# First transfers, layer seam and constants of a four-layer graph network reordered on one core

## Chip, cores and metric

The kernel runs on one core of a Trainium2 chip. The metric is the device time of one execution in microseconds (us), as the median of several executions. All arithmetic is 32-bit float.

## The reference, cut to what matters

128 graphs of 64 nodes with 256 features pass through four layers. Each layer's output is added to its input and the sum is layer-normalised.

```python
x = LN(x + L0(x, adj))    # 5 node groups: two graph convolutions 256 -> 512 -> 256, weighted by a softmax
x = LN(x + L1(x, adj))    # one graph convolution, 256 -> 256
x = LN(x + L2(x, adj))    # polynomial of degree 3 in the row-normalised adjacency, leaky relu
x = LN(x + L3(x, adj))    # 5 steps of a gated recurrent unit over A = (adj != 0)

# L0, per group g with its nodes idx (25, 9, 7, 6 and 6 of the 64):
A = adj_g + I;  An = dinv * A * dinv
h = relu(An @ (x_g @ W1[g]) + b1[g])
fused[idx] += w[g] * relu(An @ (h @ W2[g]) + b2[g])
# L3: agg = A^T (h W_l);  h = GRU(agg, h)   for l in 0..4
```

## The kernel before

Layer 0 works on 8 batches of 16 graphs. Layers 1 to 3 work on 16 chunks of 8 graphs. Layer 0's result of a chunk goes through DRAM (`x1`). The engines' transfers are issued in order, each by the queue of the engine that the call names (`nc.sync`, `nc.scalar`, `nc.gpsimd`).

```python
def load0(s):                                 # 18 adjacency and 12 row transfers per batch
    for t, (g, b0, nb) in enumerate(TILES):
        for f, n in RUNS[g]:
            for fc, m in RUNS[g]:
                nc.sync.dma_start(a0[s % 2][rows, t, col : col + m], adj[b, f : f + n, fc : fc + m])
            nc.sync.dma_start(xg[rows, t, :], x[b, f : f + n, :])
    # ... two 512 KB tiles xt of the inputs for the residual, on nc.sync
loaded = {0: load0(0)}
# ... ident, eye0, block0, b1 on nc.scalar
for g in range(NG):                           # 10 x 512 KB of weights
    nc.scalar.dma_start(W1[:, g], ...)
    nc.gpsimd.dma_start(W2[:, g], ...)
# ... b2, fusion weights fw on nc.sync

# prep(s):   ae = a0 + eye, degrees, A0 (VectorE); transposes pT; gathers pa0 -> ag0
# groups(s): hidden(g): ph -> hg;  support(g): ps -> s2;  add(g): po -> F (fusedT)
# residual(s): transposes pse of F, xt += pse, layernorm, store to x1
for _ in prep(0):
    pass
for s in range(NS):
    beside = []
    if s:
        beside.append(residual(s - 1))
    if s + 1 < NS:
        loaded[s + 1] = load0(s + 1)
        beside.append(prep(s + 1))
    interleave(*beside, groups(s))            # one step of each in turn
interleave(residual(NS - 1))

# after layer 0, in its memory: loads of chunks 0 and 1 (a64, xt), constants, then
interleave(both(mid(0), mid(1)), fold())      # mid: layers 1 and 2 of a chunk; fold: recurrent weights
for c in (0, 1):
    rows.append(Chunk(c)); rows[c].state_of_layer2(); rows[c].messages()
for s in range(NCH * L):                      # the recurrent loop, mid(c) of later chunks as filler
    ...
```

Of the kernel before, what the change touches and what calls it, by code (L numbers as in the profile page):

```python
# [43 lines left out]
def gnn_stack(  # L44
# [29 lines left out]
    small = ctx.enter_context(tc.tile_pool(name="small", bufs=4))  # L74
    dram = ctx.enter_context(tc.tile_pool(name="dram", bufs=1, space=bass.MemoryType.DRAM))
# [60 lines left out]


    with ExitStack() as c0:
        w0 = c0.enter_context(tc.tile_pool(name="w0", bufs=1))
        work = c0.enter_context(tc.tile_pool(name="work0", bufs=1))  # L140
        pt = c0.enter_context(tc.tile_pool(name="pt0", bufs=8, space=PSUM))

        def psum(name):
            return pt.tile([128, 512], F32, tag="pt", name=name)
# [6 lines left out]
        nc.gpsimd.memset(A0, 0.0)  # L151

        def load0(s):
            xg = work.tile([TR, NT, D], F32, name="xg", bufs=2)
            for t, (g, b0, nb) in enumerate(TILES):
                b = slice(s * SB + b0, s * SB + b0 + nb)
                row = 0
                for f, n in RUNS[g]:
                    rows = slice(row, row + nb * n)
                    row += nb * n  # L160
                    col = 0
                    for fc, m in RUNS[g]:
                        nc.sync.dma_start(a0[s % 2][rows, t, col : col + m], adj[b, f : f + n, fc : fc + m])
                        col += m
                    nc.sync.dma_start(xg[rows, t, :], x[b, f : f + n, :])
            xt = []
            for c in (2 * s, 2 * s + 1):
                t = work.tile([128, NP, D], F32, name="xt0", bufs=4)
                nc.sync.dma_start(t, xv[c])
                xt.append(t)  # L170
            return a0[s % 2], xg, xt

        loaded = {0: load0(0)}

        ident = const(c_ident, [128, 128], "ident", nc.scalar)
        eye0 = const(c_eye0, [TR, NT, NJ], "eye0", nc.scalar, w0)
# [4 lines left out]
        for g in range(NG):  # L181
            nc.scalar.dma_start(W1[:, g], w1[g].rearrange("(k p) e -> p k e", p=128))
            nc.gpsimd.dma_start(W2[:, g], w2[g].rearrange("(k p) e -> p k e", p=128))
        b2c = const(b2.rearrange("g (k p) -> p (g k)", p=128), [128, NG * 2], "b2", pool=w0)
# [22 lines left out]
        def prep(s):  # L207

            a, xg, xt = loaded.pop(s)
# [25 lines left out]
            for t0 in range(0, NT, 4):  # L235
                n = min(4, NT - t0)
                p = psum("pT")[:TR, : n * TR].rearrange("p (t n) -> p t n", t=n)
# [8 lines left out]
            for ts, o, w in ((range(4), 0, half), (range(4, NT), half, NC0 - half)):  # L246
                for k in range(2):
                    p = psum("pa0")
# [8 lines left out]
            ready[s] = AT, ag0, xt  # L257

        def groups(s):

            AT, ag0, xt = ready.pop(s)
# [6 lines left out]
            def hidden(g):  # L268
                _, o, w = at(g)
                hg = work.tile([128, 4, w], F32, name="hg0" if g == 0 else "hg", bufs=1 if g == 0 else 2)  # L270
                for e in range(4):
                    p = psum("ph")[:, :w]
# [7 lines left out]
            def support(g):  # L280
                ts, o, w = at(g)
                hg, s2 = hgs.pop(g), []
                for u in range(0, len(ts), 2):
                    tu = ts[u : u + 2]
                    p = psum("ps").rearrange("p (t d) -> p t d", t=2)
# [12 lines left out]
            def add(g):  # L298
# [3 lines left out]
                for k in range(2):  # L302
                    p = psum("po")[:, :w]
# [23 lines left out]
            ready[s, "x"] = xt  # L327

        def residual(s):
            for c, xt in zip((2 * s, 2 * s + 1), ready.pop((s, "x"))):  # L330
                for t in range(NP // 2):
                    p = psum("pse").rearrange("p (q d) -> p q d", q=2)
# [15 lines left out]
        for s in range(NS):  # L348
            beside = []
            if s:  # L350
                beside.append(residual(s - 1))
            if s + 1 < NS:
                loaded[s + 1] = load0(s + 1)
                beside.append(prep(s + 1))
            interleave(*beside, groups(s))
# [4 lines left out]
    pg = ctx.enter_context(tc.tile_pool(name="pg", bufs=5, space=PSUM))  # L360
    pt = ctx.enter_context(tc.tile_pool(name="pt", bufs=3, space=PSUM))

    def psum(name):
        return pt.tile([128, 512], F32, tag="pt", name=name)

    def load(c):
        a64 = work.tile([128, NP, N], F32, name="a64", bufs=2)
        nc.sync.dma_start(a64, av[c])
        xt = work.tile([128, NP, D], F32, name="xt", bufs=5)
        nc.sync.dma_start(xt, x1[c])  # L370
        return a64, xt

    loaded = {0: load(0), 1: load(1)}

    pair = const(c_pair, [128, 2, N], "pair", nc.scalar)
    cw = spread(conv_w, 4, "cw")
    cb = spread(conv_b, 1, "cb")
    l1bs = spread(l1b, D, "l1bs")
    L1W = const(l1w.rearrange("(k p) e -> p k e", p=128), [128, 2, D], "L1W")
    L2W = const(l2wT.rearrange("(k p) e -> p k e", p=128), [128, 2, D], "L2W")  # L380
    bih = const(bihT, [128, 6], "bih")
    bhh = const(bhhT, [128, 6], "bhh")
    mask = const(maskT, [128, B // 2], "mask")
    brz = wp.tile([128, 4], F32, name="brz")
    nc.vector.tensor_add(brz, bih[:, 0:4], bhh[:, 0:4])


    cI = wp.tile([128, 3, 128], F32, name="cI")
    for k in range(3):
        nc.vector.tensor_scalar(cI[:, k, :], ident, cw[:, k : k + 1], None, op0=ALU.mult)  # L390
# [3 lines left out]
    V = [wp.tile([128, 3, 7, 128], F32, name=f"V{l}") for l in range(L)]  # L394
    WHH = wp.tile([128, 3, 7, 128], F32, name="WHH")
# [8 lines left out]
    def fold():  # L404
        st = work.tile([128, 4, 2, D], F32, tag="RZ", name="ih", bufs=2)
        whh = work.tile([128, 2, 3 * D], F32, tag="NI", name="whh", bufs=2)
        for q in range(3):
            nc.gpsimd.dma_start(st[:, q], wihT[:, q * D : (q + 1) * D].rearrange("(k p) e -> p k e", p=128))
        nc.gpsimd.dma_start(whh, whhT.rearrange("(k p) e -> p k e", p=128))
        wl = work.tile([128, 4, 2, D], F32, tag="RZ", name="wl", bufs=2)  # L410
        wls = [wl[:, l] for l in range(4)] + [st[:, 3]]
        for l in range(L):
            nc.gpsimd.dma_start(wls[l], wlT[l].rearrange("(k p) e -> p k e", p=128))
        yield
# [6 lines left out]
        for l in range(L):  # L421
            for q in range(3):
                p = psum("pf").rearrange("p (j e) -> p j e", j=2)
                for j in range(2):
                    for k in range(2):
                        nc.tensor.matmul(
                            p[:, j, :], wls[l][:, k, j * 128 : (j + 1) * 128], st[:, q, k, :], start=k == 0, stop=k == 1
# [62 lines left out]
    def gather(src, m, name, tag="ag"):  # L490

        a = work.tile([128, 2, NP * 128], F32, tag=tag, name=name, bufs=2 if tag == "agg" else 1)
        for k in range(2):
            p = psum("pa")
            for q in range(NP):
                nc.tensor.matmul(  # L496
                    p[:, q * 128 : (q + 1) * 128], src[:, q, k * 128 : (k + 1) * 128], m[:, q, :], start=True, stop=True
                )
            nc.scalar.copy(a[:, k, :], p)  # L499
        return a  # L500

    state = {}

    def mid(c):

        a64, xt = loaded.pop(c)


        Ab = work.tile([128, NP, 128], F32, name="Ab", bufs=1)
        nc.vector.tensor_mul(  # L510
            Ab.rearrange("p q (b m) -> p q b m", b=2),
            a64[:, :, None, :].to_broadcast([128, NP, 2, N]),
            pair[:, None, :, :].to_broadcast([128, NP, 2, N]),
        )
        A01 = work.tile([128, NP, 128], F32, name="A01", bufs=4)
        nc.vector.tensor_scalar(A01, Ab, 0.0, None, op0=ALU.not_equal)
        rsum = small.tile([128, NP], F32, name="rsum")
        nc.vector.tensor_reduce(rsum, a64, AX.X, ALU.add)
        rdeg = small.tile([128, NP], F32, name="rdeg")
        nc.vector.tensor_scalar(rdeg, rsum, 1.0, None, op0=ALU.add)  # L520
        rinv = small.tile([128, NP], F32, name="rinv")
        nc.vector.tensor_scalar(rinv, rsum, 1e-9, None, op0=ALU.add)
        nc.vector.reciprocal(rinv, rinv)
        dinv1 = inv_sqrt(rdeg, NP, 128, "d1")
        A1 = work.tile([128, NP, 128], F32, name="A1", bufs=1)
        nc.vector.tensor_add(A1, Ab, ident[:, None, :].to_broadcast([128, NP, 128]))
        nc.vector.tensor_mul(A1, A1, dinv1[:, :, None].to_broadcast([128, NP, 128]))
        nc.vector.tensor_mul(Ab, Ab, rinv[:, :, None].to_broadcast([128, NP, 128]))
        yield


        AT1 = work.tile([128, NP, 128], F32, name="AT1", bufs=1)
        p = psum("pT1").rearrange("p (q n) -> p q n", q=NP)
        for q in range(NP):
            nc.tensor.transpose(p[:, q, :], A1[:, q, :], ident)
        nc.vector.tensor_mul(AT1, p, dinv1[:, :, None].to_broadcast([128, NP, 128]))

        poly = work.tile([128, NP, 128], F32, tag="poly", name="poly3", bufs=2)
        p = psum("pT2").rearrange("p (q n) -> p q n", q=NP)
        for q in range(NP):  # L540
            nc.tensor.transpose(p[:, q, :], Ab[:, q, :], ident)
        nc.vector.scalar_tensor_tensor(
            poly, p, cw[:, 3:4], cI[:, 2, None, :].to_broadcast([128, NP, 128]), op0=ALU.mult, op1=ALU.add
        )
        yield
# [139 lines left out]
    def both(*gens):  # L685
        for g in gens:
            yield from g
# [120 lines left out]
```

## Time and profile before

| | before |
|---|---|
| median (lowest to highest of 3) | 2464.16 us (2463.45 to 2464.48) |
| span of the profiled run | 2462.4 us, mean granted clock 0.986 |
| busy share | TensorE 93%, VectorE 53%, ScalarE 44%, GpSimd 23% |
| first transposes of batch one / batch two | 38.99 us / 61.73 us |
| layer 0 in the middle (61.73 to 338.66) | 276.9 us |
| seam: last batch to the loop's first gate product (338.66 to 484.80) | 146.1 us, TensorE busy 104.1 |
| recurrent loop (from 484.80) | 1977.6 us |

The last four rows cut the span at batch two's transposes, the last batch and the loop, without gaps. The granted clock is TensorE's clock in the profile as a share of full speed. TensorE's idle time lies densest at the start (38.99 and 4.36 us) and in the seam (42.0 of 146.1 us). The loop has 86.3 us of it in 1977.6, which the change does not aim at. The lines behind the table are shown in the prediction.

### The profile page before, as it was taken

Reading aid. Unit: us, or ns where it says so; the run is one execution under the profiler, and the core shown is the slowest. Engines: PE = TensorE matmul, PEld = TensorE weight load, DVE = VectorE, ACT = ScalarE, POOL = GpSimd, SP = SyncE. Lnnn points to the kernel's source line nnn. Section 1 sums busy time; section 2 is a strip of 40 time slices with the busy share of each in tenths; the row PEclk is TensorE's granted clock in tenths of the full one; section 3 lists DMA queues with packets and bytes.
Section 4 is the critical chain, followed back from the end, with each engine's and each line's share of the span. In section 5 each row is a group of like instructions: output and inputs, shape, how many; then the busy total and the mean of one; then the engine's idle time right before and its main releaser. Section 6 shows DMA issues by size and latency. Waiting matters only on the chain.

```text
span 2462.4 us, 31767 instructions
## 1 busy us (share of the span) xinstructions
PE 2281.0 (93%) x12288; PEld 1994.1 (81%) x12288; DVE 1315.6 (53%) x2914; ACT 1090.6 (44%) x2102; POOL 567.0 (23%) x606
## 2 busy tenths in 40 slices
PE   2999994999999999999999999999999999999996
PEld 2878783788888888888888888888888888888885
DVE  1333324555566556655565556555655565555445
ACT  1343441444444444444445444545454545454443
POOL 1101002322222222222222222222132222222221
PEclk9999996999999999999999999999999999999998
DMA  5222113000000000000000000000000000000000
GB/s 157 67 79 88 50 44 116 3 3 1 3 18 20 1 3 18 20 1 3 18 20 1 3 18 20 1 3 16 22 1 1 9 18 1 1 3 16 1 1 17
DMA packets 55318, 54.34 MB, mean 22 GB/s; under 512 B 24224, under 2 KB 48512, under 8 KB 55168
## 3 DMA queue, kind: packets, MB, share of 16 engines
q1 hardware_dynamic: 51616, 43.74, 5.6%
q0 software_dynamic: 1504, 5.51, 0.6%
q10 hardware_dynamic: 2048, 3.06, 0.4%
q8 instruction: 97, 1.59, 0.3%
q14 instruction: 53, 0.43, 0.1%
HBM read 35.52 MB, written 16.78 MB: 21 GB/s over the span
## 4 chain that ended last, share of the span: by engine, by line
PE 53%; DVE 29%; ACT 9%; POOL 3%; issue 3%; DMA 2%; SPq 1%; DVEq 0%; POOLq 0%; ACTq 0%
PE parz L460 9%; PE pan L460 6%; PE pa L496 6%; PE ps L289 5%; PE pdrz L460 4%; PE pbrz L460 4%; DVE RZ L653 4%; DVE RZ L654 4%; PE ph L274 4%; DVE hn L655 3%; DVE NI L647 2%; DVE NI L648 2%; ACT NI L652 2%; DVE RZ L482 2%; PE pbn L460 2%
## 5 line engine op out<-in xcount | busy, mean ns | idle before, releaser
L476 ACT COPY c<-parz 128x512 f32<-128x512 f32 x240 | 140.4, 585 | 369.9 <-PE parz L460 369.9
L460 PE MATMUL parz<-Th,WHH 128*128 128x256 f32 x960 | 285.9, 379 | 0.0
L460 PE MATMUL parz<-Ta,V 128*128 128x256 f32 x960 | 285.5, 379 | 0.0
L440 POOL TENSOR_TENSOR Th<-hn 128x512 f32<-128x512 f32 x64 | 93.5, 1461 | 653.5 <-DVE hn L655 653.5
L652 ACT ACTIVATE NI<-NI,bih 128x512 f32<-128x512 f32 x160 | 115.5, 722 | 224.4 <-DVE NI L648 224.4
L460 PEld LDWEIGHTS parz<-Ta,V 128*128 128x128 f32 x960 | 182.4, 190 | 24.8
L476 ACT COPY c<-pan 128x512 f32<-128x512 f32 x240 | 141.0, 587 | 125.9 <-PE pan L460 125.1
L440 POOL TENSOR_TENSOR Ta<-agg 128x512 f32<-128x512 f32 x80 | 101.5, 1269 | 400.8 <-ACT agg L499 400.8
L460 PEld LDWEIGHTS parz<-Th,WHH 128*128 128x128 f32 x960 | 176.0, 190 | 21.2 <-ACT c L476 0.5
L478 DVE TENSOR_TENSOR NI<-pdn,c 128x512 f32<-128x512 f32 x80 | 54.8, 684 | 229.8 <-ACT c L476 229.8
L460 PE MATMUL pan<-Ta,V 128*128 128x256 f32 x480 | 147.4, 389 | 20.9 <-ACT c L476 19.7
L625 ACT ACTIVATE RZ<-RZ,brz 128x512 f32<-128x512 f32 x160 | 106.4, 712 | 128.0 <-DVE RZ L488 128.0
L107 POOL TENSOR_TENSOR rs<-ve,mhalf 128x4 f32<-128x4 f32 x64 | 64.5, 1008 | 413.6 <-DVE ve L105 401.7
L460 PE MATMUL pan<-Th,WHH 128*128 128x256 f32 x480 | 143.7, 381 | 0.0
L482 DVE TENSOR_TENSOR NI<-pbn,c 128x512 f32<-128x512 f32 x80 | 55.3, 692 | 149.9 <-PE pbn L460 149.4
L496 PEld LDWEIGHTS pa<-A,h 128*128 128x128 f32 x1024 | 123.7, 192 | 13.9 <-ACT h L669 11.0
L113 ACT ACTIVATE xt<-xt,nb,rs 128x256 f32<-128x256 f32 x192 | 99.7, 589 | 75.3 <-DVE nb L110 75.3
L496 PE MATMUL pa<-A,h 128*128 128x128 f32 x1024 | 125.5, 276 | 7.7 <-ACT h L669 7.6
L289 PE MATMUL ps<-W,hg 128*100 128x256 f32 (+3 forms) x576 | 131.8, 381 | 0.0
L596 PE MATMUL pT<-ident,hn 128*128 128x128 f32 x640 | 96.5, 277 | 25.9 <-DVE hn L655 25.9
L596 PEld LDWEIGHTS pT<-ident,hn 128*128 128x128 f32 x640 | 74.2, 141 | 48.5 <-PE pT L596 34.3
L289 PEld LDWEIGHTS ps<-W,hg 128*100 128x100 f32 (+3 forms) x576 | 91.0, 163 | 27.2
(183 smaller groups left out, 5214.4 us busy)
## 6 DMA issues: line engine op xcount, KB each, us to landing
xt<-in_x_dram SPq DMA_DIRECT2D x16, 512.0 KB
x<-xt SPq DMA_DIRECT2D x16, 512.0 KB
xt<-x SPq DMA_DIRECT2D x16, 512.0 KB
out_dram<-xt SPq DMA_DIRECT2D x16, 512.0 KB
xg<-in_x_dram SPq DMA_DIRECT2D x32, 100.0 KB
W<-in_w_dram POOLq DMA_DIRECT2D x5, 512.0 KB, 9.2
W<-in_w_dram ACTq DMA_DIRECT2D x5, 512.0 KB
a<-in_adj_dram SPq DMA_DIRECT2D x16, 128.0 KB
```

The costliest lines, as they stand in the source:

```text
L113: nc.scalar.activation(y[:, p, :], y[:, p, :], AF.Identity, bias=nb[:, p : p + 1], scale=rs[:, p : p + 1])
L274: nc.tensor.matmul(p, W1[:, g, k, e * 128 : (e + 1) * 128], ag0[:, k, o : o + w], start=k == 0, stop=k == 1)
L289: nc.tensor.matmul(p[:r, h, :], hg[:, e, TOFF[t] - o : TOFF[t] - o + r], W2[:, g, e, :], start=e == 0, stop=e == 3,)
L440: nc.gpsimd.tensor_sub(t[:, 0:2, :], a[:, :, H:], a[:, 0, :].rearrange("p (s n) -> p s n", s=2))
L460: nc.tensor.matmul(bank[:, g, :], w[:, q, i - 1, :], rhs, start=i in (1, 2, 5) and g == 0 and m == 0, stop=m == len(side) - 1, skip_group_ ...
L476: nc.scalar.copy(c, self.a)
L482: nc.vector.tensor_add(C[:, :, 0, :H], b, self.copies.pop(1))
L496: nc.tensor.matmul(p[:, q * 128 : (q + 1) * 128], src[:, q, k * 128 : (k + 1) * 128], m[:, q, :], start=True, stop=True)
L596: nc.tensor.transpose(p[:, q * 128 : (q + 1) * 128], src(q, k), ident)
L625: nc.scalar.activation(RZ[:, q, 0, :], RZ[:, q, 0, :], AF.Sigmoid, bias=b[0])
L652: nc.scalar.activation(n, n, AF.Tanh, bias=bih[:, 4 + j : 5 + j])
L653: nc.vector.tensor_sub(d, self.hT[:, j, :], n)
```

## The change

Its intent has three parts. Batch one's transfers go out first, on three queues, and the weights follow on the sync queue. Layers 1 and 2 of the first two chunks run beside layer 0's last batch. The constants and the recurrent weights are fetched during layer 0, into memory of their own. The diff, with moved code and renamings cut:

```diff
+    keep = ctx.enter_context(tc.tile_pool(name="keep", bufs=1))    # mid, load, gather moved up and into keep
+    pg = ...(name="pg", bufs=5, space=PSUM)                        # PSUM: 8 buffers become 5 + 3
+    pt = ...(name="pt", bufs=3, space=PSUM)
...
         def load0(s):
+            qa = [nc.scalar, nc.sync] if s == 0 else [nc.sync]
+            qx = nc.gpsimd if s == 0 else nc.sync
...
-                        nc.sync.dma_start(a0[s % 2][rows, t, col : col + m], ...)
+                        qa[i % len(qa)].dma_start(a0[s % 2][rows, t, col : col + m], ...)
-                    nc.sync.dma_start(xg[rows, t, :], x[b, f : f + n, :])
+                    qx.dma_start(xg[rows, t, :], x[b, f : f + n, :])
...
         for g in range(NG):
-            nc.scalar.dma_start(W1[:, g], ...)
-            nc.gpsimd.dma_start(W2[:, g], ...)
+            nc.sync.dma_start(W1[:, g], ...)
+            nc.sync.dma_start(W2[:, g], ...)
+        xts = {0: load_x(0)}
...
             if s + 1 < NS:
                 packed[s + 1] = load0(s + 1)
+                xts[s + 1] = load_x(s + 1)
                 beside.append(prep(s + 1))
+            if s == 1:
+                pair = const(..., nc.gpsimd)        # and cw, cb, l1bs; L1W, L2W, bih, bhh, mask on nc.gpsimd
...
+            elif s == 3:                            # wihT, whhT, wlT: 9 transfers, 2.8 MB, on nc.gpsimd
+                nc.gpsimd.dma_start(ih[:, q], ...)
...
+            elif s == NS - 1:
+                for c in (0, 1):
+                    loaded[c] = load(c)
+                beside.append(both(mid(0), mid(1)))
             interleave(*beside, groups(s))
...
-        interleave(both(mid(0), mid(1)), fold())
+        weights = fold()
         for c in (0, 1):
+            for _ in range(6):
+                next(weights)
             rows.append(Chunk(c))
             ...
+        for _ in weights:
+            pass
```

## The prediction

> **What bounds the kernel now.** I read the table of busy time by stretch first, cut at the instructions that begin and end the stages, then the waits of TensorE in the bad stretch, then the timeline around its edges. The columns of the first are: stretch in us, its length, busy time of TensorE's matmuls, its weight loads, VectorE, ScalarE and GpSimd (instructions in brackets), granted TensorE clock, DMA share, GB/s.
>
> ```profile
> 0.00:38.99 38.99, 0.00 (x0) 0.03 (x1) 2.92 (x11) 0.00 (x0) 8.62 (x12) 1.00 0.65 197
> 38.99:61.73 22.74, 18.39 (x77) 14.99 (x78) 5.47 (x24) 7.43 (x14) 1.80 (x1) 0.99 0.31 89
> ...
> 338.66:374.22 35.56, 34.34 (x205) 27.97 (x205) 10.79 (x37) 14.84 (x36) 2.01 (x2) 1.00 0.07 30
> 374.22:484.80 110.58, 69.78 (x360) 61.79 (x361) 60.94 (x196) 31.05 (x86) 30.66 (x42) 0.80 0.19 66
> 484.80:2462.40 1977.60, 1891.28 (x9954) 1665.10 (x9952) 1141.32 (x2304) 922.43 (x1694) 501.04 (x532) 0.99 0.03 9
> ```
>
> The recurrent loop (from 484.80, 80% of the span) has TensorE busy 1891 of 1978 us. The change does not touch its instructions, so 1977.6 us stay. Layer 0 between 61.73 and 374.22 is just as full (34.3 of 35.6 us in its last batch). What is to be had lies in two places: the start, where TensorE does nothing for 38.99 us, and the seam from 374.22 (layer 0's last transposes) to 484.80 (first gate product of the loop), where it is idle for 40.8 us of 110.6 and its mean clock is 0.80.
>
> TensorE's waits in the seam (engine, tile and line, whom it waited for: total us, times, longest):
>
> ```profile
> PE pT L535 <- DVE d1z L89: 19.8, 1, 19.8
> PE pa L496 <- ACT xt L113: 11.6, 2, 6.7
> PE pa L496 <- DVE AT L536: 7.6, 2, 7.3
> PE pp L550 <- DVE poly L552: 1.8, 2, 0.9
> ```
>
> The 19.8 us are layer 0's last layernorm, its store, then the loads of the first chunk and the weights, which only now have room. The 11.6 us are the two layernorms of layer 1, on which the second gather depends, and there is little else for TensorE to do.
>
> The timeline at the start (start us, length, engine, what, and the idle time before it):
>
> ```profile
> 5.45 19.96 ACTq L182 DMA_DIRECT2D W<-in_w_dram  x5
> ...
> 34.50 0.40 DVE L211 TENSOR_TENSOR ae<-a,eye 112x225 f32<-112x225 f32 x1 [33.12 <-DMA a<-in_adj_dram]
> ...
> 38.99 1.90 PE L239 MATMUL pT<-ident,A 112*112 112x112 f32 x9 [38.99 <-DVE A L219]
> ...
> 57.23 0.40 DVE L211 TENSOR_TENSOR ae<-a,eye 112x225 f32<-112x225 f32 x1 [14.61 <-DMA a<-in_adj_dram]
> ...
> 61.73 1.90 PE L239 MATMUL pT<-ident,A 112*112 112x112 f32 x9 [4.36 <-DVE A L219]
> ```
>
> The first batch's 30 small transfers share the engines with 5.2 MB of weights and are there at 34.50. The second batch's 30 follow on the sync queue from 36.97 and are there at 57.23: 20.3 us for 0.9 MB, one issue per 0.65 us, so the queue's issuing sets this. TensorE had finished the first batch's hidden layer at 57.37 and waited 4.36 us for batch two's transposes, although batch one's next products were ready.
>
> **What the Trainium skill says.** "TensorE: Matmul & The Clock Gate", Part 1 (the HAM clock gate): the array's clock falls to half after an idle window of some 3.4 us and comes back after a busy one. The trace agrees: after the 19.8 us wait the gather of 16 matmuls took 3.78 us, after a wait of 4.95 us 3.98 us, and 2.05 us where TensorE had been busy. The same page, Part 2, Step-by-step: matmuls stay in program order; only weight loads are pulled ahead. The 4.36 us above agree, so I let TensorE follow the program. "DMA: Bandwidth & Descriptors", Issuing engines are not separate DMA queues: transfers from several issuers run on the same 16 DMA engines, so a second issuer saves issue time only. The page calls that usually small; here it is 20 us for a batch, so three queues do help batch one, but the bytes of the weights must still pass.
>
> **The change, part by part.**
>
> *Start.* Batch one: 9 adjacency issues each on two queues at 0.65 us (5.9 us from 0.75), 12 row issues on GpSimd at some 0.75 us (its weight issues took 0.748 us). Landing takes about 1.5 us (last issue of batch two ended at 55.8, the sum began at 57.23), with a weight transfer possibly ahead. The sum could begin near 11, the transposes 4.5 us later as before (34.50 to 38.99), delayed by GpSimd, which now clears a tile after its 12 issues: near 16. The hidden layer began 9.5 us after the transposes and ended 8.9 us later, so TensorE is through with it at 34 to 36 instead of 57.37. That would be 22 us won.
>
> But batch two's transposes come next in the program, and batch two's transfers stand on the sync queue behind all weights and two input tiles. Bytes ahead: 10 x 512 KB and 2 x 512 KB are 6.3 MB, batch one's rows 0.87 MB, constants 0.36 MB, together 7.5 MB. The DMA engines moved 350 GB/s where they were full (10 to 15 us), so 21.5 us, from about 2 us on: done at 24. I choose that 6 of batch two's 30 issues are out by then; 24 x 0.65 = 15.6 us makes 39.6, plus 1.5 to land and 4.5 to the transposes: 46. TensorE idles about 11 us where it idled 4.36, and **61.7 becomes about 46: 15.5 us won, not 22.**
>
> *Seam.* The two chunks' layers 1 and 2 move beside layer 0's last batch. Their TensorE work at full clock, from the second chunk's groups: transposes 1.0, gathers 2 x 2.05, polynomial 2 x 1.15, linear layers 2 x 3.62: 14.7 us each, 29.4 for both. Stage from 338.66, summed anew: the last batch 35.6 (it has no next batch to prepare), plus 29.4. Waits that stay, in program order: after each first linear layer comes only one piece of layer 0 (1.9 us) before the second gather, but the layernorm takes 6.7 us (415.7 to 422.4, 448.8 to 455.4), so 2 x 4.8; the polynomial 2 x 0.9; two half-clock gathers 2 x 1.9; 1 for other things: 16 us. Then the last transposes 1.9, the folded weights 15 x 1.75 = 26.2 (40 matmuls took 8.80 us), both chunks' transposes and gathers 5.6 (479.23 to 484.80). Sum 114.7 against 146.1 before (338.66 to 484.80). I take off 1.5 for PSUM, as layer 0's eight buffers are now 5 and 3, the 3 shared with the moved work: **30 us won.**
>
> *Constants.* The small ones already went out at 144 to 148 us, in layer 0, so moving them gives nothing. The 2.8 MB of recurrent weights, which had to wait at 389 for layer 0's memory, now come 200 us early; that gain is in the seam's sum (the weights are resident when the folding begins). GpSimd pays 9 issues at 0.75 us, beside 44 us stages that use 2 to 6 us of it: hidden.
>
> Total 45.5 of 2464.2: **2419 us**, 1.8% less.
>
> **Rivals.** (a) The start wins all: if batch two is there by 36, because the sync queue pushes it between the weights, 25 us are won and the time is about 2409. Against it: the queue is served in order and its issue rate is seen. (b) The start wins nothing: the weights crawl as from 15 to 30 us, when the same DMA engines ran half full at 148 to 218 GB/s; then they end at 35, batch two at 58, and the time is 2434. For it: that stretch; against it: there the weights competed with 100-row transfers on their own queue, and only one weight queue ran. (c) The moved work fits better: if TensorE's order fills the layernorm waits, the seam wins 41 us, and the time is 2408. Against it: the order above shows no such filling. (d) VectorE becomes the bound in the last batch: it has 10.8 us there and would take some 40 more in about 80, so no, but its queue may lengthen each layernorm by 1 to 3 us and cost 2 to 6: 2424.
>
> **Range and chances.** Start 15.5 give or take 6, seam 30 give or take 6, taken as independent: give or take 8.5, and a little wider for the order of the queues, which I cannot see. 8 in 10: 2404 to 2435. The 2% line is 2414.9, that is 49.3 us won; I stand 4 us short of it, so faster by over 2% has 0.33, within 2% 0.65, slower 0.02.
>
> **What would show it.** First transposes near 16 us and batch two's near 46 with about 11 us of idle time before them, ended by VectorE after an adjacency transfer. Weights landed by about 24 at 340 GB/s or more. From the last batch's first transposes to the first gate product about 116 us, with two waits of 4 to 5 us of the second gathers on ScalarE's layernorm, and no wait near 20 us. The clock at 1.00 in the folding. The loop 1977 us long, within 3. The prediction is wrong if batch two's transposes are no later than batch one's hidden layer, if the weights' transfer is slower, or if the loop itself moves.

## The result, and the profile after

| | before | after |
|---|---|---|
| median (lowest to highest of 4) | 2463.80 us (2461.78 to 2464.48) | 2432.17 us (2431.15 to 2432.88) |
| ratio to before | | 0.9873 (95%: 0.9856 to 0.9890) |
| span of the profiled run, mean clock | 2462.4 us, 0.986 | 2429.4 us, 0.987 |

A ratio is the mean time of one kernel's fast runs over that of the other's of the same rounds, so it is not quite the ratio of the medians. The kernel is 1.3% faster, within 2%, and the time lies inside the stated range, 13 us above the stated 2419.

The table of busy time by stretch of the kernel after has the columns of the prediction's first view. It is cut at the same events: both first transposes, the last batch, layer 0's last transposes, the loop.

```profile
0.00:19.77 19.77, 0.00 (x1) 0.03 (x1) 2.93 (x11) 1.28 (x1) 13.90 (x22) 1.00 0.70 168
19.77:62.93 43.16, 18.56 (x77) 15.09 (x78) 5.72 (x25) 5.59 (x13) 10.05 (x14) 0.76 0.70 227
62.93:341.68 278.75, 269.50 (x1700) 225.58 (x1701) 99.34 (x370) 114.73 (x272) 26.25 (x21) 0.98 0.22 70
341.68:413.63 71.95, 62.74 (x377) 54.04 (x377) 41.36 (x122) 27.77 (x60) 7.18 (x8) 0.95 0.10 34
413.63:453.16 39.53, 37.14 (x185) 32.42 (x185) 27.99 (x81) 18.01 (x60) 23.93 (x32) 0.91 0.15 54
453.16:2429.40 1976.24, 1890.09 (x9953) 1664.69 (x9951) 1142.19 (x2308) 921.84 (x1696) 494.19 (x524) 1.00 0.03 9
```

The first transposes begin 19.2 us earlier, at 19.77 instead of 38.99. Batch two's begin at 62.93 instead of 61.73, so **all of that is gone one stage later**. The second line shows it: of 43.16 us TensorE is busy 18.56. Booked by piece, before to after:

| piece | before | after | difference | predicted |
|---|---|---|---|---|
| to batch two's transposes | 61.73 | 62.93 | +1.2 | -15.5 |
| to the last batch | 276.93 | 278.75 | +1.8 | 0 |
| seam | 146.14 | 111.48 | -34.7 | -30 |
| loop | 1977.60 | 1976.24 | -1.4 | 0 |
| sum (spans) | 2462.4 | 2429.4 | -33.0 | -45.5 |

TensorE's waits of the kernel after before the loop (whom it waited for: total us, times, longest):

```profile
PE pT L365 <- DVE A L345: 44.4, 2, 24.6
PE pse L461 <- DVE d1s L94: 6.5, 1, 6.5
PE pa L157 <- ACT xt L116: 5.5, 2, 4.3
PE pse L461 <- DVE fusedT L445: 4.6, 2, 3.5
PE pf L543 <- ACT w L550: 2.1, 1, 2.1
```

The first line is the start: 19.77 us before batch one and 24.60 before batch two. The second line is new. The third is what is left of the two layernorm waits of 11.6 us, and the wait of 19.8 us at the seam is gone.

Where the 24.60 us come from is in the timeline of the transfers' issues and of the instructions that wait for them (kernel after; start us, length, engine, line, what, count, idle time before it):

```profile
1.25 10.15 ACTq L284 DMA_DIRECT2D a<-in_adj_dram  x9
1.25 11.73 SPq L284 DMA_DIRECT2D a<-in_adj_dram  x9
...
18.39 0.79 POOL L82 DMA_DIRECT2D L1W<-in_l1w_dram  x1
...
22.43 11.08 SPq L294 DMA_DIRECT2D xt<-in_x_dram  x2
...
26.34 2.88 POOL L508 DMA_DIRECT2D wl<-in_wlT_dram  x4 [0.39 <-DMA L2W<-in_l2wT_dram]
...
35.87 0.68 SPq L284 DMA_DIRECT2D a<-in_adj_dram  x1
...
58.40 0.40 DVE L337 TENSOR_TENSOR ae<-a,eye 112x225 f32<-112x225 f32 x1 [14.37 <-DMA a<-in_adj_dram]
```

Three things are to be seen. First, two queues need 10.15 and 11.73 us for 9 adjacency issues each, so 1.1 to 1.3 us for one, where one of batch two's in the kernel before took 0.65. The weights after the first stand behind these issues on the sync queue, and the second weight leaves only at 13.03. Second, GpSimd's queue sends `L1W` at 18.39 and `wl` at 26.34, with the other later weights between. The program names them in its second and fourth stage (`s == 1`, `s == 3`), but nothing made these issues wait, and they were placed as early as they could go. Third, the sync queue's two `xt` issues take 11.08 us, so batch two's first issue leaves at 35.87 and its last near 57.

The view of the DMA queues between 13 and 36 us says how much that was (packets, MB, share of the 16 engines):

```profile
q1 hardware_dynamic: 3426, 4.29, 56.3%
q0 software_dynamic: 946, 3.13, 37.4%
```

The second line is GpSimd's queue: 3.13 MB of constants and weights of layers 1 to 3, which TensorE first uses after 341 us (3.5 MB were issued in all; the rest moved after 36 us). In this stretch 333 GB/s are moved, so by this estimate they cost 3.13 MB / 333 GB/s = 9.4 us of full DMA engines. By 5 us slices the DMA share is 1.02 to 1.07 all the way from 15 to 40 us; in the kernel before it was 0.48 to 0.71 from 15 to 30 us.

The new wait is shown by these lines of the kernel after:

```profile
178.97 0.52 SPq L146 DMA_DIRECT2D a<-in_adj_dram  x1
181.29 0.42 DVE L180 TENSOR_REDUCE rsum<-a 128x4 f32<-128x256 f32 x1 [8.66 <-DMA a<-in_adj_dram]
182.87 1.94 PE L461 MATMUL pse<-ident,fusedT 128*128 128x128 f32 x8 [6.47 <-DVE d1s L94]
```

The adjacency of a first chunk is issued at 178.97, behind a batch of small transfers. VectorE has the chunk's row sum next in its queue and stands for 8.66 us, although the last additions of `fusedT` are ready, and TensorE waits for those. The products then run at half clock: 1.94 us for 8 transposes that take 1.04 elsewhere. "TensorE: Matmul & The Clock Gate", Part 1 (on the array's architecture), calls ScalarE's and VectorE's queues strict first in, first out; this trace agrees. It is the moved work that put the row sum there.

### The profile page after: what moved, and what is told of

Its sections match the earlier page's. It is cut to its first block, busy times and chain, and to the rows that moved or that the text cites. A ratio compares the mean times of both kernels' runs of the same rounds, so it can differ in the third digit from the quotient of the medians.

```text
span 2429.4 us, 31756 instructions
## 1 busy us (share of the span) xinstructions
PE 2278.0 (94%) x12288; PEld 1991.8 (82%) x12288; DVE 1319.5 (54%) x2914; ACT 1089.2 (45%) x2102; POOL 575.5 (24%) x619
## 4 chain that ended last, share of the span: by engine, by line
PE 53%; DVE 29%; ACT 9%; POOL 3%; issue 3%; DMA 2%; SPq 1%; ACTq 0%; DVEq 0%; POOLq 0%
PE parz L577 9%; PE pan L577 7%; PE pa L157 6%; PE ps L415 5%; PE pdrz L577 5%; PE pbrz L577 4%; DVE RZ L674 4%; DVE RZ L675 4%; PE ph L400 3%; DVE hn L676 3%; DVE NI L668 3%; DVE NI L669 2%; ACT NI L673 2%; ACT xt L116 2%; DVE RZ L599 2%
## 5 line engine op out<-in xcount | busy, mean ns | idle before, releaser
L617 PEld LDWEIGHTS pT<-ident,hn 128*128 128x128 f32 x640 | 74.3, 142 | 48.8 <-PE pT L617 34.7
```

The source lines that it names most:

```text
L617: nc.tensor.transpose(p[:, q * 128 : (q + 1) * 128], src(q, k), ident)
```

## The experiments

The theory (A): the start's gain was used up by transfers ahead of batch two, of which 3.1 MB belong to later stages, and the new wait is a VectorE held by a late transfer. Rivals for the start: (B) the queues' issuing alone is the limit, so bytes do not matter; (C) TensorE stands only because its order puts batch two's transposes first. For the seam: either the early fetch or the place of the work wins it. Twelve kernels ran, each in 4 executions beside 7 of the kernel before. All outputs are right. The edits are cut to the lines that matter.

| run | median us | ratio to before | batch two's transposes at | loop starts at |
|---|---|---|---|---|
| change | 2432.17 | 0.9873 | 62.93 | 453.16 |
| e1 later weights behind batch two | 2414.11 | 0.9800 | 53.04 | 434.43 |
| e2 one adjacency queue | 2432.15 | 0.9873 | 63.70 | 452.58 |
| e3 batch two amid the weights | 2415.90 | 0.9805 | 52.47 | |
| e4 chunk adjacency on GpSimd | 2423.66 | 0.9838 | 64.19 | |
| e5 layers 1 and 2 after layer 0 | 2442.96 | 0.9910 | 61.71 | 463.59 |
| e6 start alone | 2455.23 | 0.9961 | 53.90 | 478.21 |
| e7 = e1 + e3 + e4 | 2410.79 | 0.9781 | 42.65 | 431.87 |
| e8 = e1 + preparation later | 2409.26 | 0.9772 | 62.90 | 429.95 |
| e9 = e8 + rows on GpSimd | 2406.13 | 0.9756 | 69.67 | 428.47 |
| e10 = e9 + e4 | 2411.97 | 0.9779 | 69.59 | 434.48 |
| e11 = e9 + fusion weights earlier | 2405.50 | 0.9748 | 70.52 | 427.70 |
| e12 = e9 + fusion weights first | 2408.16 | 0.9771 | 72.68 | 426.37 |

The 95% intervals of the ratios are 0.0014 to 0.0022 to each side. From e8 on batch two's transposes come late by design. e1 to e4 ran on one chip, e5 to e8 on one, e9 and e10 on one, e11 and e12 each on one of its own.

### e1: the later weights behind batch two

```diff
-                L1W = const(..., "L1W", nc.gpsimd)     # likewise pair, L2W, bih, bhh, mask, ih, whh, wl
+                L1W = const(..., "L1W", nc.sync)
```

> The changed kernel, but the constants and the later layers' weights (3.1 MB, which in its trace went out on the GpSimd queue from 13 to 30 us, long before the stage in which they are written down) go on the sync queue, where they stand behind batch two. Theory A, their bytes hold up layer 0's weights: batch two's first transposes come 3.1 MB / 0.36 MB per us = 8.7 us earlier, 62.9 to about 54, and the kernel takes about 2423 us. Rival B, only the order on the sync queue counts: the first transposes stay at 62 to 63 and the time at 2432.

Batch two's first issue left at 26.47 instead of 35.87. The timeline has for the `xt` issues on the sync queue and for TensorE:

```profile
21.91 2.81 SPq L294 DMA_DIRECT2D xt<-in_x_dram  x2
...
53.04 1.90 PE L365 MATMUL pT<-ident,A 112*112 112x112 f32 x9 [14.20 <-DVE A L345]
```

The transposes came 9.9 us earlier, about the 9.4 us of bytes worked out above, as (A) says and (B) excludes. The two `xt` issues took 2.81 us instead of 11.08, so most of these microseconds are the ones that they had held the sync queue; they are not a second loss. Of the 14.20 us that remain (B) is right in part: batch two's 30 issues now ran from 26.47 to 47.8, 21.4 us. The time fell by 18 us, not 10, and was 9 us below the theory's 2423: from these transposes to the loop it was 381.4 us instead of 390.2, as the 6.5 us wait at 182.87 and its half clock were gone too. That was not intended. The order of the sync queue had changed, which is the likely reason, not tested by itself.

### e2: one queue for batch one's adjacency

```diff
-            qa = [nc.scalar, nc.sync] if s == 0 else [nc.sync]
+            qa = [nc.sync]
```

> The changed kernel, but all 18 adjacency transfers of batch one on the sync queue instead of 9 on it and 9 on ScalarE's. In the changed kernel each of the 9 took 1.13 to 1.30 us where one queue alone takes 0.65 us. Theory A, the two queues share what issues them: the 18 still end near 13 us, the sum over the adjacency begins within 1 us of 15.3, and the time stays at 2432 within 3 us. Rival B, they issue side by side and were slow for another reason (the first weight ahead of them, the row transfers of GpSimd): the 18 end near 20 us or later, and the sum begins 5 us or more later.

```profile
1.24 15.06 SPq L284 DMA_DIRECT2D a<-in_adj_dram  x18
```

One queue issued all 18 in 15.06 us (0.84 us each), two needed 11.73. The adjacency was there 3.4 us later (sum from 18.70 instead of 15.28), which is neither what the theory nor what its rival gave; a miss in size. Batch two's transposes moved from 62.93 to 63.70 and the time not at all. The second queue is worth 3.3 us of issuing, and nothing of the time in this kernel.

### e3: batch two's transfers between the weights

```diff
         for g in range(NG):
+            if g == 2:
+                packed[1] = load0(1)
             nc.sync.dma_start(W1[:, g], ...)
```

> The changed kernel, but batch two's 30 transfers go out after the weights of the first two groups instead of after all weights and two input tiles. Theory, batch two's place in the sync queue sets the start: 13 us + 4 weight issues 2 us + 30 x 0.65 us = 34.5, landed at 36 to 37, transposes 4.5 us later near 41 instead of 62.9, TensorE idle before them 3 us instead of 24.6, time near 2432 - 21 = 2411. Rival, the DMA engines are full with weights whatever the order (10.6 MB at 0.36 MB per us are 30 us): the small transfers crawl among them and the transposes come at 50 or later, time 2420 or more.

Batch two's first issue left at 14.25, but the 30 issues took until 47.2 us, not 20 us. The timeline of the sync queue, with a single issue of 2.87 us and a gap of 3.3 us behind the next:

```profile
28.97 2.87 SPq L287 DMA_DIRECT2D xg<-in_x_dram  x1
31.88 1.53 SPq L284 DMA_DIRECT2D a<-in_adj_dram  x2
36.72 0.31 SPq L287 DMA_DIRECT2D xg<-in_x_dram  x1
```

The transposes came at 52.47, where the theory had 41. Being early in the queue helped only in part while the DMA engines were full of other transfers: GpSimd's 3.1 MB were still sent in this run, and without them (e7) the same 30 issues took 23 us. The 6.5 us wait had gone here as well, so 16 us were won.

### e4: the chunks' adjacency by GpSimd's queue

```diff
-        nc.sync.dma_start(a64, av[c])
+        nc.gpsimd.dma_start(a64, av[c])
```

> The changed kernel, but the chunks' adjacency for layers 1 and 2 is fetched by GpSimd's queue instead of the sync queue. In the changed kernel VectorE stood 8.7 us before a sum over such a tile (the transfer was issued at 179 us, behind 90 others) and TensorE lost 6.5 us behind it at 183 us. Theory, that stall costs its 6.5 us in full: time 2425 to 2427, and no wait over 2 us of TensorE between 64 and 340 us. Rival, TensorE makes it up or another wait takes its place: 2430 to 2433.

This aims at the new wait alone. From batch two's transposes (themselves after 24.9 us) to 340 us TensorE's only listed wait was:

```profile
PE pse L461 <- DVE fusedT L445: 1.2, 1, 1.2
```

The time fell by 8.5 us, 1.3 us below the theory's range, with the start 1.3 us later (64.19). From batch two's transposes to the loop some 9.5 us were won: the 6.47 of wait, the half clock after it, and a wait of 1.36 us at 151.91 that had gone as well. So the mechanism of the new wait is shown: VectorE's queue was held by that transfer.

### e5: layers 1 and 2 of the first chunks after layer 0 again

```diff
-                beside.append(both(mid(0), mid(1)))
...
+        interleave(both(mid(0), mid(1)), fold())
```

> The changed kernel with one thing undone: the first chunks' layers 1 and 2 run after layer 0 again, beside the folding of the weights, but their inputs, constants and the recurrent weights are still fetched early. Theory: the larger half of the seam's 34.7 us comes from the early fetch (the 19.8 us wait for the last layernorm, its store and the loads goes), and only some 10 to 14 us from the place of the work: about 2444 us (2440 to 2448), with the waits of the second gathers for the layernorm back at 9 to 13 us in all. Rival: the place beside layer 0 is what wins: 2455 us or more.

TensorE's waits in this run's seam:

```profile
PE pa L157 <- ACT xt L116: 10.2, 2, 5.2
PE pa L157 <- DVE AT L198: 7.0, 2, 6.7
```

2442.96 us, the theory within 1 us. The seam lasted 122.5 us (341.05 to 463.59): 23.6 less than before, 11.1 more than after. So, booked in this order, **two thirds of the seam's gain come from fetching early, a third from the place of the work**. The layernorm waits are back at 10.2 us, and so is the wait of 7.0 for the chunk's transposed adjacency.

### e6: the start alone, on the kernel before

The edit is the diff's `load0`, weights and `load_x` parts, without the other two parts.

> The kernel before with the change of the start alone (three queues, weights behind them on the sync queue), so without the 3.1 MB of later weights that were fetched ahead of batch two. Theory (those bytes ate the start's gain): batch two's transposes at 52 to 55 us instead of 61.7, time 2454 to 2457 us, 7 to 9 less than before. Rival (the start wins nothing in any case): transposes at 60 to 63, 2462 to 2465 us.

```profile
53.90 1.90 PE L246 MATMUL pT<-ident,A 112*112 112x112 f32 x9 [14.60 <-DVE A L226]
```

7.3 us were won, and batch two's transposes came at 53.90 as (A) says. So the change of the start is worth 7 us by itself, and the parts disturb each other: the early fetch of the recurrent weights took it back.

### e7: three edits at once

e1, e3 and e4 together.

> The changed kernel with three edits at once: later weights and constants on the sync queue behind batch two, batch two's transfers behind the weights of groups 0 and 1, chunk adjacency on GpSimd's queue. Theory (the gains add): batch two's transposes at 43 to 48 us, time 2403 to 2410 us. Rival (batch two's small transfers crawl among the weights whatever else is there): transposes at 50 to 53, 2411 to 2416 us, no better than one edit alone.

```profile
42.65 1.23 PE L367 MATMUL pT<-ident,A 112*112 112x112 f32 x9 [2.70 <-DVE A L347]
...
161.59 1.94 PE L463 MATMUL pse<-ident,fusedT 128*128 128x128 f32 x8 [6.16 <-DVE d0z L92]
```

With the 3.1 MB away, the early issues did get through (14.36 to 37.4 us), and TensorE waited 2.70 us instead of 14.20. But the loop began only 2.6 us earlier than in e1. At 161.59 a wait of 6.16 us had come back, this time for a batch's own adjacency: TensorE had caught up with the sync queue. The theory's time was missed by 1 us; the transposes came before its 43 to 48 and far from the rival's 50 to 53.

### e8: batch two's preparation later in the program

```diff
-                beside.append(prep(s + 1))
+                beside.append(both(iter([None] * (14 if s == 0 else 0)), prep(s + 1)))   # on e1
```

> The late-weights kernel (2414 us) with one more edit: in the first stage, the preparation of batch two comes 14 steps later in the program, so TensorE reaches batch two's transposes only after most products of batch one. Theory (the idle time is one of order: TensorE stands before batch two's transposes although batch one's products are ready): the 14.2 us wait there goes, batch three's transposes begin near 83 us instead of 94, time 2400 to 2405 us. Rival (the weights are not there either): the wait turns into one for the weights of groups 1 to 6, batch three's transposes at 90 us or later, 2410 to 2415 us.

This tests (C). TensorE went through batch one's products from 28.70 to 62.90 without a listed wait and began batch three's transposes at 78.07 instead of 94.15: 16 us won there, so (C) is true as well. At the loop's start 4.5 us were left. The rest went here:

```profile
119.14 7.07 PE L415 MATMUL ps<-W,hg 128*100 128x256 f32 x32
128.33 2.90 PE L377 MATMUL pa<-AT,xg 100*128 100x100 f32 x16 [2.12 <-issue]
```

Two slices of 2 us after that wait, in the columns of the stretch view (the last three are granted clock, DMA share and GB/s):

```profile
130.00:132.00 2.00, 2.00 (x11) 2.00 (x11) 1.53 (x9) 0.54 (x2) 0.64 (x1) 0.50 1.09 369
...
142.00:144.00 2.00, 2.00 (x8) 1.20 (x7) 0.00 (x0) 0.00 (x0) 0.00 (x0) 0.78 0.29 96
```

TensorE stood 2.12 us while the DMA engines were full (share 1.06 in that slice), and the clock then stayed at 0.50 for some 14 us although it was busy, until the second of these slices. The four groups of products from 128.33 to 144.38 took 16.7 us; in a full-clock stage the same groups took 9.9 (1.93, 1.96, 2.38 and 3.62). With 2.1 and 3.6 us of waits (the latter at 202 us) that is 12.5, about the 11.6 us that are missing. Neither theory's time was met.

### e9: all row transfers on GpSimd's queue

```diff
-            qx = nc.gpsimd if s == 0 else nc.sync
+            qx = nc.gpsimd                            # on e8
```

> The prep-later kernel (2409 us) with the row transfers of every batch on GpSimd's queue instead of the first batch's only, so that the sync queue has 18 issues per batch and not 30. Theory (what it won at the start is given back because TensorE now catches up with the sync queue, which issues nearly without a gap until 158 us): the waits of 2.1 us at 128 and 3.6 us at 202 and the half-clock stretch from 128 to 144 go, 8 to 12 us in all: 2397 to 2402 us. Rival (the later batches wait for the bytes, or GpSimd's own work is delayed by issuing): no gain or a loss, 2407 to 2414 us, with new waits of the transposes for VectorE.

The waits at 128 and 202 us and the half-clock stretch were gone, as the theory says. Yet the time fell only to 2406.13, between the two ranges (ratio 0.9756 against 0.9772 on another chip; the intervals overlap, so a gain over e8 is not shown). A new wait stood in the first batch:

```profile
42.45 0.16 DVE L315 TENSOR_REDUCE fm<-fw 128x1 f32<-128x5 f32 x1 [20.56 <-DMA fw<-in_fusion_w_dram]
...
43.48 8.89 PE L415 MATMUL ps<-W,hg 128*100 128x256 f32 x28 [4.84 <-ACT hg L403]
```

The 2.5 KB of fusion weights came at 42 us. ScalarE's exponential of them stood ahead of six activations of the hidden layer.

### e10: e9, and the chunks' adjacency on GpSimd

> The same, and the chunks' adjacency on GpSimd's queue too. Theory: what is left of the wait near 202 us (VectorE held by the chunk's adjacency) goes; if the rows alone already removed it, the time is that of the rows alone within 2 us. Rival: GpSimd's queue is now the late one, 3 us or more slower than the rows alone.

5.8 us slower than e9. The rival's result, but by another way than it said: the chunk's adjacency came so early that its VectorE work (from 69.34 on) was done ahead of batch two's `AT`, for which TensorE then waited 5.31 us (the wait at 43 us was 6.07 here instead of 4.84):

```profile
75.79 0.62 DVE L366 TENSOR_TENSOR AT<-pT,d0o 112x448 f32<-112x448 f32 x1
...
76.46 7.99 PE L377 MATMUL pa<-AT,xg 100*128 100x100 f32 x36 [5.31 <-DVE AT L366]
```

The mean clock between 60 and 100 us was 0.83. The edit that gave 8.5 us in e4 costs time here.

### e11 and e12: the fusion weights earlier

```diff
-        fw = spread(fusion_w, NG, "fw", w0)           # sync queue, behind the weights
+        fw = const(..., [128, NG], "fw", nc.scalar, w0)   # e11: after ScalarE's other constants
```

In e12 the new line stands ahead of `eye0`, so that it is the first issue of all.

> The kernel with the rows on GpSimd (2406 us) with the 2.5 KB of the fusion weights fetched by ScalarE's queue before the layer's weights, not by the sync queue behind them. Theory: in that kernel TensorE's wait of 4.84 us at 43.5 comes from ScalarE's in-order queue, held before the exponential of the fusion weights by that transfer (issued at 29.62, used at 42.45); with it gone the wait and the half clock after it go, 6 to 8 us: batch three's transposes near 78, about 2399 to 2401 us. Rival: the next wait (batch two's adjacency, or ScalarE on something else) takes its place, 2404 us or more.

> As the last one, but the 2.5 KB of fusion weights are the very first issue of ScalarE's queue, before the eye constant and batch one's adjacency. In the last run they stood behind these, and VectorE, whose program has their first use ahead of batch one's normalisation, waited 6.67 us for them, so that the first transposes began at 26.96 instead of 19.3. Theory: both waits are gone, first transposes at 19 to 21 us, batch three's near 78, 2397 to 2401 us. Rival: with the start 7 us earlier TensorE meets the later batches' transfers again, as with the preparation placed later: 2403 us or more, with new waits after 100 us.

The wait at 43 us was gone in both, and it had moved to the front. Two lines of VectorE's timeline, first of e11, then of e12:

```profile
23.23 0.16 DVE L315 TENSOR_REDUCE fm<-fw 128x1 f32<-128x5 f32 x1 [6.67 <-DMA fw<-in_fusion_w_dram]
```

```profile
28.44 0.17 DVE L325 TENSOR_TENSOR gb<-b,gw 128x10 f32<-128x10 f32 x1 [10.58 <-DMA b<-in_b_dram]
```

In e11 VectorE waits for the fusion weights ahead of batch one's normalisation, in e12 for the next constant of the same computation (`b2`, 5 KB). The first transposes began at 26.96 and 29.83 instead of 19.33. The time is that of e9 within the intervals (0.9748 and 0.9771), so the rivals were right on the time; for e12 they had expected new waits after 100 us, and there were none above 1.2 us until the seam. e9 and e11 are the best versions, 2.4 to 2.5% faster than before and some 26 us faster than the change by the medians (29 to 31 by the ratios, as they ran on other chips).

## Why the prediction was right or wrong

**The time and its range** held, at 13 us from the middle, because a large error and small ones partly cancel: the start was forecast 16.7 us too good, the seam 4.7 too bad, the middle of layer 0 1.8 too good, the loop 1.4 too bad. This is luck in part: with the seam and the loop as forecast the time would have been about 2438, outside 2404 to 2435.

**The start: the step that failed** is "Bytes ahead ... together 7.5 MB", moved "from about 2 us on: done at 24", with "I choose that 6 of batch two's 30 issues are out by then". None was out before 35.87. Its own sign failed too: the weights had not landed by 24, as the sync queue issued the last of them at 21.84 and the DMA engines stayed full to 40. Two terms of this sum were mis-sized. The bytes lacked the 3.1 MB on GpSimd's queue, which the constants' paragraph had at "200 us early" and "hidden": 9.4 us by bytes, 9.9 by e1. And the DMA engines were not full "from about 2 us on" but from 15 (70 to 144 GB/s before 13 us, about 300 and more after 15), because nine of the ten weights stood behind the adjacency issues on the sync queue. These were put at "5.9 us" for 9 on each of two queues and took 10.15 and 11.73: issuing on two queues at once was slower for each, and e2 puts the whole use of the second queue at 3.3 us. This second term also made the first transposes 19.77 instead of "near 16". It is read from the trace; no run tests its cost for batch two alone, and in e2 3.3 us more of it moved batch two by 0.8 us only. Without the 3.1 MB the first issue of batch two left at 26.47 (e1), where the forecast implies about 20 (6 issues of 0.65 us out by 24), and the start alone gives 53.90 (e6), still 8 us short of the stated 46.

**What was right there**: that TensorE follows the program and stands before batch two's transposes although batch one's products are ready. e8 shows that this order, not the lack of work, costs 14 us in e1. Rival (b)'s time, 2434, is within 2 us, but not by its path: it had "batch two at 58" (62.93 was measured) and the DMA engines half full, and they were full from 15 to 40 us. Its two numbers do not fit each other either, since 58 instead of 61.7 makes about 2430.

**The seam**: the mechanism held (no wait near 20 us, both linear layers beside the last batch), and the size was off by 4.7 us. The term is "Waits that stay ... 16 us", above all "2 x 4.8" for the layernorms. They measured 1.14 and 4.33. "No such filling" was wrong: layer 0's hidden products and additions stood ahead of the second gather in TensorE's order, which is half of rival (c). Idle time in the seam fell from 42.0 us (146.14 less 104.12 busy) to 11.6 (111.48 less 99.88), and busy time by 4.2 us, with the mean clock up from 0.85 to 0.94. "1.00 in the folding" was wrong: the mean clock was 0.91 there, after waits of 3.46 and 2.14 us. One reading behind the clock's part was off: the gather of 3.78 us stood after a wait of 7.30 us for `AT` (405.19 in the kernel before), not directly after the 19.8 us wait.

**Constants**: "gives nothing" held for the small ones. The early fetch as a whole, the chunks' inputs included, carried two thirds of the seam's gain (e5), and its weights took away the start's (e1).

**VectorE**: rival (d) looked for a delay in the last batch. It came at 182.87 us instead, from an instruction that waits for a transfer. That was not foreseen, and with the residual's shorter waits (1.18 us in most stages before, one stage after) it leaves +1.8.

**The loop** held: 1976.2 against 1977.6.

What stays open: why two queues slow each other's issues (even one queue took 0.84 us for each of batch one's in e2, not 0.65), and why the clock stayed low for 14 us in e8. What the start could give without any of these waits was not reached: e8, e9, e11 and e12 each removed one and met the next.

## What to carry to other kernels

A transfer written late in the program isn't late if nothing holds it: list what every queue really sends in the stretch that matters, and add up those bytes, before crediting an early start. A start that is made earlier only counts at the next point where TensorE needs a transfer, so book the span by stages and look where the gain is given back. Before an engine with an in-order queue waits for a small constant or a chunk's load, ask which ready work stands behind it; moving the transfer alone often only moves the wait.

## What the Trainium skill lacked or had wrong

- "DMA: Bandwidth & Descriptors", Issuing engines are not separate DMA queues, says that issuing from several engines saves only the sequencer's time and that this is usually small. The runs agree that only issue time is saved: 18 issues took 15.06 us on one queue and 11.73 on two. What the page lacks is that the saving is far from half, since each issue rose from 0.84 to 1.13 and 1.30 us, and that a batch of 30 small transfers costs 20 us of issuing (20.3 us in the kernel before).
- The same page, Rules for kernel authors, advises to issue a transfer early and wait late. It lacks the other side: 3.1 MB of weights issued 340 us and more before TensorE used them delayed what was needed next by 9.9 us (e1), as the DMA engines were full (share 1.02 to 1.07).
- "TensorE: Matmul & The Clock Gate", Part 1: the clock is said to fall after an idle window of some 3.4 us and to come back after a busy one as long. In e8 a listed wait of 2.12 us was followed by some 14 us at 0.50 while TensorE was busy, and in the kernel after one of 2.14 us (before 431.25) by 3.4 us at 0.50; waits of 2.11 us in e2 (before 153.08) and 2.49 us in e3 (before 185.38) left the clock at 1.00. So in these traces the length of the listed wait alone does not tell whether the clock falls. Some records of a trace can be missing, so these are observations and no rule.
- No page has it: the granted clock column can read 1.00 at the start of a trace while the instructions run at half speed. In the kernel after, the first 9 transposes took 1.90 us at a listed clock of 1.00 and 1.03 us later; the lengths, not the clock column, tell the half clock at the start.
